# Leads per batch: another order for the same instructions in a four-layer graph network

## The chip, the cores and the metric

The kernel runs on one core of a Trainium2 chip. The core has five engines that this document names by their short forms: PE (TensorE, matrix multiplications; PEld is its weight load), DVE (VectorE), ACT (ScalarE), POOL (GpSimd) and SP (SyncE, which here issues most DMAs). Each engine works through its own list of instructions in the order in which it was written, and waits on semaphores for the others. The metric is the device time of one execution in microseconds (us): the median of several runs. A difference of 0.2% (about 5 us) is about the smallest that a measurement of this kernel can tell from none.

## The reference

Sixteen graphs (batches) of 1024 nodes with 128 features pass through four layers. Each layer normalises its input, applies a ReLU, runs a graph operation on the dense 1024 x 1024 adjacency matrix `adj`, and adds the result to its input `x`. All is in float32.

```python
# layer 0, three times (i = 0, 1, 2):
h = h @ W + b;  nh = h / norm(h);  cos = nh @ nh.T
h = (edge_weight * cos) @ h;  h = relu(h)          # no relu after the last
# layer 1:
y = relu(((1 + eps) * x + adj.T @ x) @ W1 + b1) @ W2 + b2
# layer 2: attention from two scores per node
alpha = tanh(s1[:, None] + s2[None, :]);  h = softmax(where(adj > 0, alpha, -1e15)) @ h
# layer 3: attention from h A h' (made symmetric), softmax over rows, then three gates
e = (h @ A) @ h.T;  e = e + e.T;  att = softmax(where(adj > 0, e, 0), axis=1) * adj
hp = relu(att @ h);  out = o * tanh(sigmoid(i * hp + f * x))
```

The products `cos` and `e` are symmetric: the kernel computes their upper blocks and mirrors the rest.

## The kernel before, in words

**Tiling.** The 1024 nodes are 8 blocks of 128 partitions; a half (columns 0 to 511 or 512 to 1023) fills one PSUM bank of 512 float32. For every batch, `turn` loads the adjacency as eight tiles `adjT`: the DMA brings 32 x 32 squares to their mirrored places (L880), DVE transposes within the squares (L888), ACT sums the rows (L891). Layer 1 also loads the plain rows (`adjL`).

**A square product.** In layers 0 and 3, `Square.row(j, s)` makes row block j of the product for half s in a PSUM tile `sq`: matmuls for the upper blocks (L761), and PE transposes of kept blocks for the lower ones (L771). `Square.keep` puts the upper blocks into `above`: on ACT (a copy, L793), or, for batches 1 to 13, on DVE for rows 0 to 3 of the second half (L783). In the latter case `send` writes the blocks to HBM (`by_hbm`) and reads them back transposed as `got`, which replaces the PE transposes of rows 4 to 7 in the first half. DVE then multiplies each half by the adjacency (`ew` in layer 0, L960; `e` in layer 3, L1178), and PE accumulates over j (`acc`, L823, or L834 where the nodes are wanted on partitions). In layer 3, a row also needs its maximum (L1190), an exponential on ACT (L1194) and a second multiplication by the adjacency (L1203) first.

**Between products** there are short chains over several engines: a projection `psP` (PE), a bias or scaling (DVE), a transpose `ps_hTn` (PE) and its eviction (ACT, L623); and in front of each layer a normalisation: statistics (DVE, L671, L680), a reciprocal root (POOL, L563), scaling of half the blocks on DVE (L699) and half on ACT (L706), transposes `ps_hT` or `ps_hnT` (PE). The last part of layer 3, `finish`, is a chain of gates; its two tanh passes over z are L1275 and L1276.

**What sets the order.** The kernel first registers all operations of all batches with a planner, `Plan`, each with engine, planned duration, batch, and the tiles that it reads and writes. `link` adds dependencies (two engines that touch one PSUM bank count as dependent, reads included) and gives every operation a rank: the due time of its batch (60 us apart, the last one 52), less the longest planned path behind it (`tail`), less a **lead**. `order` then replays the program: it takes the engine that can start something first and, of what that engine could start within 0.05 us of that, the operation of lowest rank. A larger lead so moves an operation forward in its engine's list and a smaller one moves it back. At most two batches beyond the oldest one may be under way on the engines, and the numbers of tiles are limited (POOLS, KINDS). The instructions are written in the resulting order, engine by engine, and are fixed from then on: on the chip, an engine does not pass over one that waits. The planner's durations are its own and are used for the order alone.

Operations form groups by a key: stage, engine, and the first tile written, such as "3 ACT z" (layer 3, ACT, tile z) or "00 ACT above" (layer 0, first product). Before the change, LEADS holds one lead for a group, and may hold others for the first two batches ("<0", "<1") and the last two (">1", ">0"): 551 numbers. Batches 2 to 13 share the group's lead.

**The constants.** `prepare` loads the parameters of the later layers through ACT's DMA queue, in pieces between other ACT work, and computes a few matrices from them; the second and third products of layer 0, and layer 1, wait for it.

Of the kernel before, what the change touches and what calls it, by code (L numbers as in the profile page):

```python
# [53 lines left out]
class Plan:  # L54
# [53 lines left out]
    def link(self):  # L108
# [23 lines left out]
        for o in reversed(self.ops):  # L132
            o.tail = o.us + max((s.tail + o.lat for s in o.succs), default=0.0)
            lead = self.leads.get(o.key + o.edge, self.leads.get(o.key, 0.0))
            o.rank = (self.deadline(o.batch) - o.tail - lead, o.seq)
# [87 lines left out]
def tile_adj_preln(  # L223
# [30 lines left out]
    B = x.shape[0]  # L254
# [71 lines left out]
    for load_it in first:  # L326
# [19 lines left out]

    LEADS = {
        "0 ACT hT": -1, "0 DVE hn": -8, "0 DVE mv": 42.5, "0 DVE nb": -20, "0 DVE st": -77.5, "0 PE ps": -72.5,
        "0 POOL rstd": -1, "00 ACT above": -10.5, "00 ACT hT": 95, "00 ACT hTn": -20.5, "00 ACT sq": -31,
        "00 DMA by": -13.5, "00 DMA got": 15.5, "00 DVE above": -135, "00 DVE ew": 79.5, "00 DVE h": -95.5,  # L350
        "00 DVE ss": -131.5, "00 PE acc0": -252.5, "00 PE ps": -142, "00 PE psP": -0.5, "00 PE sq": -18.5,
        "00 POOL rn": -129.5, "01 ACT above": 56, "01 ACT hT": 11.5, "01 ACT hTn": 15, "01 ACT sq": 15.5,
        "01 DMA by": 4.5, "01 DMA got": 18.5, "01 DVE above": 4.5, "01 DVE ew": 51.5, "01 DVE h": -2.5,
        "01 DVE ss": 16, "01 PE acc0": -164.5, "01 PE ps": 42, "01 PE psP": -5.5, "01 PE sq": -11,
        "02 ACT above": -2, "02 ACT hTn": -615, "02 ACT sq": -25.5, "02 DMA by": 63.5, "02 DMA got": 0.5,
        "02 DVE above": 43.5, "02 DVE ew": -232.5, "02 DVE ss": 79.5, "02 DVE x": -55.5, "02 PE acc0": -28.5,
        "02 PE ps": 12.5, "02 PE sq": 222, "02 POOL rn": -103, "1 ACT g": -33, "1 ACT hn": 66, "1 ACT y1": -7.5,
        "1 DMA adjL": -113, "1 DVE adjL": -21, "1 DVE hn": 1.5, "1 DVE mv": 237.5, "1 DVE nb": 46,
        "1 DVE st": -625.5, "1 DVE x": -0.5, "1 PE acc1": 4, "1 PE py": -167.5, "1 PE py2": 67,
        "1 POOL rstd": -43, "2 ACT e2": -24, "2 ACT h": 287.5, "2 ACT hfl": 53, "2 ACT hn": -13.5,  # L360
        "2 ACT hnT": 18, "2 ACT s1": -14, "2 DVE alone": -51.5, "2 DVE e2": 48.5, "2 DVE h": 20,
        "2 DVE hn": 48.5, "2 DVE hrow": -43.5, "2 DVE mv": -2.5, "2 DVE nb": 78, "2 DVE rden": 9.5,
        "2 DVE x": 10, "2 PE acc2": 108.5, "2 PE p1": -90, "2 PE pf": -26.5, "2 PE ps": 117.5, "2 PE psP": -315,
        "2 POOL rstd": 4.5, "3 ACT above": -19.5, "3 ACT e3": 96.5, "3 ACT gate": -185.5, "3 ACT h3T": 19.5,
        "3 ACT hn": -84.5, "3 ACT hnT": -9.5, "3 ACT hp": -5, "3 ACT hpT": 41, "3 ACT hs": 46.5, "3 ACT z": 25,
        "3 DMA by": -13.5, "3 DMA got": 0.5, "3 DMA z": -130.5, "3 DVE e3": -363.5, "3 DVE gate": 83,
        "3 DVE h": -111.5, "3 DVE hn": 69, "3 DVE mv": -2, "3 DVE nb": 147, "3 DVE st": -192, "3 DVE sum": 53.5,
        "3 DVE top": -84, "3 DVE z": -925, "3 PE acc3": -130.5, "3 PE pg": -18.5, "3 PE ps": 19,
        "3 PE psN": 114, "3 PE psP": 95, "3 PE sq": -0.5, "3 POOL rstd": -59, "3 POOL z": 0.5,
        "T ACT adjT": 1.5, "T DMA adjT": -140.5, "T DVE adjT": -391, "x DMA x": 54.5, "0 ACT hT <0": -2,  # L370
        "0 ACT hT >1": -4.5, "0 ACT hn <1": -4.5, "0 DVE hn <0": 8.5, "0 DVE hn <1": 8.5, "0 DVE hn >0": 15.5,
        "0 DVE hn >1": 1, "0 DVE mv <0": -4.5, "0 DVE mv <1": 113, "0 DVE mv >0": 47.5, "0 DVE mv >1": -25.5,
        "0 DVE nb <0": 101.5, "0 DVE nb <1": -62.5, "0 DVE nb >0": -49, "0 DVE nb >1": -18.5,
        "0 DVE st <0": -85, "0 DVE st <1": -73.5, "0 DVE st >0": -122.5, "0 DVE st >1": -32, "0 PE ps <0": 85.5,
        "0 PE ps <1": 36, "0 PE ps >0": -31, "0 PE ps >1": 40, "0 POOL rstd <0": -6.5, "0 POOL rstd <1": -26,
        "0 POOL rstd >0": -7, "0 POOL rstd >1": 15.5, "00 ACT above <0": -32, "00 ACT above <1": -88,
        "00 ACT above >0": -294, "00 ACT above >1": -3, "00 ACT hT <0": 147.5, "00 ACT hT <1": -7,
        "00 ACT hT >0": 21, "00 ACT hT >1": 161.5, "00 ACT hTn <0": -70.5, "00 ACT hTn <1": 119.5,
        "00 ACT hTn >0": -22, "00 ACT hTn >1": -11, "00 ACT params <0": -26, "00 ACT sq <0": -34,
        "00 ACT sq <1": 134.5, "00 ACT sq >0": -119, "00 ACT sq >1": -25.5, "00 DMA by <1": 0,  # L380
        "00 DMA got <1": 1, "00 DVE above <1": -197, "00 DVE ew <0": 180, "00 DVE ew <1": 13,
        "00 DVE ew >0": -125, "00 DVE ew >1": -147.5, "00 DVE h <0": -25.5, "00 DVE h <1": -4.5,
        "00 DVE h >0": 12, "00 DVE h >1": -50.5, "00 DVE params <0": 171, "00 DVE ss <0": 0,
        "00 DVE ss <1": -73.5, "00 DVE ss >0": -46.5, "00 DVE ss >1": -4, "00 PE acc0 <0": -39.5,
        "00 PE acc0 <1": -212, "00 PE acc0 >0": -327.5, "00 PE acc0 >1": -253.5, "00 PE params <0": 56.5,
        "00 PE ps <0": -18.5, "00 PE ps <1": -16, "00 PE ps >0": -32, "00 PE ps >1": -130.5,
        "00 PE psP <0": -2.5, "00 PE psP <1": 32, "00 PE psP >0": -22.5, "00 PE psP >1": -43,
        "00 PE sq <0": 28.5, "00 PE sq <1": 10, "00 PE sq >0": 3.5, "00 PE sq >1": 10, "00 POOL rn <0": -11,
        "00 POOL rn <1": -164.5, "00 POOL rn >0": -96.5, "00 POOL rn >1": -144, "01 ACT above <0": 113,
        "01 ACT above <1": -11, "01 ACT above >0": 65.5, "01 ACT above >1": 24, "01 ACT hT <0": -15,  # L390
        "01 ACT hT <1": -17.5, "01 ACT hT >0": 3.5, "01 ACT hT >1": -39, "01 ACT hTn <0": 16.5,
        "01 ACT hTn <1": -22, "01 ACT hTn >0": 68, "01 ACT hTn >1": 8, "01 ACT sq <0": 174,
        "01 ACT sq <1": -3.5, "01 ACT sq >0": -69, "01 ACT sq >1": 107, "01 DMA by <1": -9, "01 DMA got <1": 25,
        "01 DVE above <1": -5, "01 DVE ew <0": 140, "01 DVE ew <1": -13.5, "01 DVE ew >0": -9.5,
        "01 DVE ew >1": -34, "01 DVE h <0": -6, "01 DVE h <1": -6, "01 DVE h >0": -4.5, "01 DVE h >1": 43.5,
        "01 DVE ss <0": -13.5, "01 DVE ss <1": 1, "01 DVE ss >0": 17.5, "01 DVE ss >1": 106,
        "01 PE acc0 <0": -17, "01 PE acc0 <1": -31, "01 PE acc0 >0": 10.5, "01 PE acc0 >1": 25.5,
        "01 PE ps <0": 46, "01 PE ps <1": 51, "01 PE ps >0": -56, "01 PE ps >1": 82, "01 PE psP >1": 6,
        "01 PE sq <0": 0, "01 PE sq <1": -6, "01 PE sq >0": 23.5, "01 PE sq >1": -25, "02 ACT above >0": -3.5,
        "02 ACT hTn <0": -145.5, "02 ACT hTn <1": -452.5, "02 ACT hTn >0": -65.5, "02 ACT hTn >1": -373.5,  # L400
        "02 ACT sq <0": -8.5, "02 ACT sq <1": -43, "02 ACT sq >0": -58, "02 ACT sq >1": -22.5,
        "02 DMA by <1": 47.5, "02 DMA got <1": 4, "02 DVE above <1": 36.5, "02 DVE ew <0": -5,
        "02 DVE ew <1": -72, "02 DVE ew >0": -202.5, "02 DVE ew >1": -44, "02 DVE ss <0": 70,
        "02 DVE ss <1": 60.5, "02 DVE ss >0": 39, "02 DVE ss >1": 58, "02 DVE x <0": -115,
        "02 DVE x <1": -125.5, "02 DVE x >0": 0, "02 DVE x >1": -173.5, "02 PE acc0 <0": -46.5,
        "02 PE acc0 <1": -209, "02 PE acc0 >0": 0, "02 PE acc0 >1": -96.5, "02 PE ps <0": -241.5,
        "02 PE ps <1": -295.5, "02 PE ps >0": -48, "02 PE ps >1": -28, "02 PE sq <0": -33.5,
        "02 PE sq <1": -145, "02 PE sq >0": 89, "02 PE sq >1": 0.5, "02 POOL rn <0": 47.5, "02 POOL rn <1": -39,
        "02 POOL rn >0": -118.5, "02 POOL rn >1": -53, "1 ACT g <0": 23, "1 ACT g <1": 48, "1 ACT g >0": 25.5,
        "1 ACT g >1": -35, "1 ACT hn <0": 57.5, "1 ACT hn <1": 189, "1 ACT hn >0": -5.5, "1 ACT hn >1": -4.5,  # L410
        "1 ACT y1 <0": 10.5, "1 ACT y1 <1": 13.5, "1 ACT y1 >0": -26.5, "1 ACT y1 >1": 10.5,
# [58 lines left out]
    now = [0, ""]  # L470

    def op(engine, us, reads, writes, fn, port=False, lat=None):
        o = plan.op(engine, us, reads, writes, fn, now[0], port, lat)
# [904 lines left out]
    params = Buf(None, [], "params")  # L1378
# [57 lines left out]
```

## Time and profile before

| what | value |
|---|---|
| time, median of 3 runs | 2437.61 us (2435.33 to 2437.78) |
| span of the profiled execution | 2440.0 us |
| PE busy | 2389.2 us |
| DVE busy | 2106.2 us |
| ACT busy | 1288.3 us |
| POOL busy | 230.9 us |
| first matmul starts | 12.9 us |
| last matmul ends by the trace | 2429.4 us |

The page of the profile cuts the span into 40 slices of 61 us and gives each engine's busy share in tenths. The groups name a line and an engine, how many instructions it has, and what ended the idle time before them. The time-ordered view gives start, duration, engine and line of each instruction, the tile written and the tiles read, and in brackets the idle time of the engine before it with the instruction that ended the wait. Buffer numbers are left out of names. In the view of waits a row reads: engine, tile and line that waited, whom it waited for; microseconds in all, number of times, longest. A float32 matmul of the program appears as two records on PE.

### The profile page before, as it was taken

To read this page: it belongs to the slowest core of one execution; us is meant where nothing else is said; L and a number is where in the kernel's file an instruction comes from. 1 tells how busy PE (TensorE), PEld (TensorE's weight loads), DVE (VectorE), ACT (ScalarE), POOL (GpSimd) and SP (SyncE) were. 2 spreads that over 40 slices of the span, in tenths; PEclk is the share of its full clock that TensorE was granted. 3 is DMA by queue.
4 is the path that set the end of the run, shared out by engine and by line. 5 is a ranking of instruction groups with operands and counts; after the bars stand their busy time and mean duration, and the time that the engine had idled before them with its cause. 6 is when DMAs were issued, how large, how long until landed. Compare 5 with 4: busy or idle time off the path is not lost. (4 is left out here: it accounts for less than half of the span.)

```text
span 2440.0 us, 34840 instructions
## 1 busy us (share of the span) xinstructions
PE 2389.2 (98%) x11946; PEld 1588.9 (65%) x11946; DVE 2106.2 (86%) x5264; ACT 1288.3 (53%) x2404; POOL 230.9 (9%) x141
## 2 busy tenths in 40 slices
PE   6999999999999999999999999999999999999996
PEld 3568576675766757576575766757676575765763
DVE  5767989888998988999889998999989888897677
ACT  4425564644646455454644646455454655656275
POOL 1100010100101001011010100101011010101021
PEclk9999999999999999999999999999999999999999
DMA  8632837559296583946739296493946738054000
GB/s 127 131 96 43 147 78 139 126 93 178 54 160 132 85 158 78 159 109 114 160 75 182 58 153 134 87 162 68 162 116 105 164 78 156 18 87 95 25 2 18
DMA packets 1129473, 263.35 MB, mean 108 GB/s; under 512 B 971856, under 2 KB 1112912, under 8 KB 1129296
## 3 DMA queue, kind: packets, MB, share of 16 engines
q1 hardware_dynamic: 1108368, 251.73, 54.9%
q10 hardware_dynamic: 20928, 9.40, 1.4%
q8 instruction: 94, 1.54, 0.3%
q14 instruction: 83, 0.68, 0.1%
HBM read 198.14 MB, written 62.91 MB: 107 GB/s over the span
## 5 line engine op out<-in xcount | busy, mean ns | idle before, releaser
L960 DVE SCALAR_TENSOR_TENSOR ew<-sq,rn,adjT 128x512 f32<-128x512 f32 x612 | 432.0, 738 | 72.1 <-ACT above L793 37.4
L823 PE MATMUL acc<-ew,h 128*128 128x512 f32 x1024 | 481.5, 597 | 3.6 <-DVE ew L960 3.6
L761 PE MATMUL sq<-hTn 128*128 128x512 f32 (+3 forms) x1152 | 431.4, 487 | 0.3 <-ACT hTn L623 0.3
L793 ACT COPY above<-sq 128x256 f32<-128x256 f32 (+3 forms) x432 | 167.8, 393 | 439.0 <-PE sq L761 239.7
L761 PEld LDWEIGHTS sq<-hTn 128*128 128x128 f32 x1152 | 200.9, 191 | 153.2 <-issue 103.5
L823 PEld LDWEIGHTS acc<-ew,h 128*128 128x128 f32 x1024 | 179.8, 192 | 164.1 <-issue 124.1
L834 PEld LDWEIGHTS acc<-h,ew 128*128 128x128 f32 x2048 | 240.7, 192 | 23.0 <-issue 17.3
L834 PE MATMUL acc<-h,ew 128*128 128x128 f32 x2048 | 250.3, 276 | 0.0
L823 PE MATMUL acc<-e,hs 128*128 128x512 f32 x512 | 242.5, 598 | 5.6 <-DVE e L1203 4.4
L834 PEld LDWEIGHTS acc<-h,e 128*128 128x128 f32 x2048 | 232.9, 192 | 11.9 <-issue 6.5
L834 PE MATMUL acc<-h,e 128*128 128x129 f32 x2048 | 233.8, 275 | 1.2 <-DVE e L1110 1.2
L823 PE MATMUL acc<-adjL,hn 128*128 128x512 f32 x512 | 233.4, 593 | 0.3 <-ACT hn L727 0.3
L563 POOL TENSOR_TENSOR rstd<-ve,mhalf 128x8 f32<-128x8 f32 x64 | 105.1, 1642 | 1249.7 <-DVE ve L682 1197.6
L1194 ACT ACTIVATE e<-e,top 128x1024 f32<-128x1024 f32 x128 | 147.0, 1149 | 135.8 <-DVE top L1190 134.4
L771 PEld LDWEIGHTS sq<-ident,above 128*128 128x128 f32 x960 | 125.8, 141 | 135.4 <-issue 89.9
L891 ACT ACTIVATE adjT<-adjT 128x1024 f32<-128x1024 f32 x128 | 135.1, 1056 | 146.0 <-DVE adjT L888 109.4
L771 PE MATMUL sq<-ident,above 128*128 128x128 f32 x960 | 175.7, 274 | 9.7 <-ACT above L793 9.7
L888 DVE STREAM_TRANSPOSE adjT<-adjT 128x1024 f32<-128x1024 f32 x128 | 155.0, 1224 | 28.2 <-DMA adjT<-in_adj_dram 21.6
L706 ACT ACTIVATE hn<-x,nb,rstd 128x128 f32<-128x128 f32 x256 | 105.3, 483 | 123.6 <-DVE nb L690 117.8
L1110 DVE SCALAR_TENSOR_TENSOR e<-adjT,e 128x512 f32<-128x512 f32 x256 | 158.7, 679 | 9.3 <-ACT e L1106 8.8
L783 DVE STREAM_TRANSPOSE above<-sq 128x512 f32<-128x512 f32 x208 | 146.5, 706 | 17.2 <-PE sq L761 17.2
L1203 DVE TENSOR_TENSOR e<-e,adjT 128x512 f32<-128x512 f32 x248 | 161.0, 680 | 0.0
(130 smaller groups left out, 3493.8 us busy)
## 6 DMA issues: line engine op xcount, KB each, us to landing
adjT<-in_adj_dram SPq DMA_DIRECT2D x512, 128.0 KB, 4.0
adjL<-in_adj_dram SPq DMA_DIRECT2D x128, 512.0 KB, 5.2
by_hbm<-above SPq DMA_DIRECT2D x104, 512.0 KB, 4.0
got<-by_hbm SPq DMA_DIRECT2D x416, 128.0 KB, 3.8
x<-in_x_dram SPq DMA_DIRECT2D x15, 512.0 KB, 4.6
out_dram<-z ACTq DMA_DIRECT2D x15, 512.0 KB, 5.6
x<-in_x_dram SPq DMA_DIRECT2D x2, 256.0 KB, 5.1
out_dram<-z ACTq DMA_DIRECT2D x2, 256.0 KB, 2.3
```

The lines of the kernel that those rows point to most:

```text
L761: lambda: nc.tensor.matmul(dst.t[:, (first - lo) * P :], cols(leftT.t, j), span(rightT.t, first, hi), start=True, stop=True),
L771: nc.tensor.transpose(cols(dst.t, r), cols(above.t, p), ident)
L783: lambda: nc.vector.transpose(span(above.t, p, p + 4), read.t),
L793: lambda: nc.scalar.copy(span(above.t, p, p + hi - first), read.t[:, (first - lo) * P :]),
L823: lambda s=s, lo=lo, hi=hi: nc.tensor.matmul(acc[s].t, cols(h.t, at, w), span(ew.t, lo, hi), start=(j == 0), stop=(j == NB - 1)),
L834: nc.tensor.matmul(a.t[:, (c - lo) * n : (c - lo + 1) * n], cols(ew.t, c), h.t[:, at * w : at * w + n], start=(j == 0 and c == lo), stop=( ...
L888: dve(V(N), [t], [t], lambda t=t: nc.vector.transpose(t.t, t.t), True)
L891: lambda t=t, c=c: nc.scalar.activation(t.t, t.t, AF.Copy, accum_out=su.t[:, c : c + 1]),
L960: lambda view=view, ew=ew, rn=rn, j=j, lo=lo, hi=hi: nc.vector.scalar_tensor_tensor(by_block(span(ew.t, lo, hi), D, 4), view(), rn.t[:, j ...
L1110: lambda e=e, j=j, lo=lo, hi=hi: nc.vector.scalar_tensor_tensor(span(e.t, lo, hi), span(aT[j].t, lo, hi), 0.0, span(e.t, lo, hi), op0=ALU. ...
L1194: lambda e=e, top=top, tot=tot: nc.scalar.activation(e.t[:, 0:N], e.t[:, 0:N], AF.Exp, bias=top.t, accum_out=tot.t),
L1203: lambda e=e, j=j, lo=lo, hi=hi: nc.vector.tensor_mul(span(e.t, lo, hi), span(e.t, lo, hi), span(aT[j].t, lo, hi)),
```

## The change

The leads are now given for each batch by itself: a group's entry is a tuple of 16 numbers, 130 groups and so 2080 numbers. The edge suffixes go, as does the field that carried them. The values were found by simulated annealing on the planner's own replays with disturbed durations: an order is sought that stays good when operations take somewhat more or less time than planned. No operation, tile, pool or planned duration changes; only the ranks do, and with them the order of each engine's list. The DMA and constant loads are ranked by the same rule.

The diff, cut to its core (the list of leads is long; two groups of it are shown, the first of them for batches 14 and 15 in the edge entries before):

```diff
-            lead = self.leads.get(o.key + o.edge, self.leads.get(o.key, 0.0))
+            lead = self.leads[o.key][o.batch] if o.key in self.leads else 0.0
             o.rank = (self.deadline(o.batch) - o.tail - lead, o.seq)
...
     LEADS = {
-        "3 ACT z": 25, ... "3 ACT z >0": -17.5, "3 ACT z >1": -24,
-        "3 ACT above": -19.5, ... "3 ACT above >0": -12, "3 ACT above >1": -124.5,
...
+        "3 ACT above": (-52.5, -66, -4.5, -49, 47, 7, -1, 36.5, 0.5, -50, 42, -6, -64.5, -64, -105.5, -0.5),
+        "3 ACT z": (-65, 31, -54.5, -78, -69, -147.5, 23, -11.5, -36.5, -108, -18, -41.5, -81.5, -46, -141.5, -27.5),
...
-        o.edge = f" <{now[0]}" if now[0] < 2 else f" >{B - 1 - now[0]}" if now[0] > B - 3 else ""
```

Two places of the resulting orders are named in what follows (line numbers of the kernel before; in the kernel after, lines below the list stand nine lower). At the head, ACT's list before is L891 of tile 6, then the copy L793 of row 5; after, the copy comes first. At the tail, ACT's list before is the two z operations of batch 14 (L1275, L1276), then the copies (L793) of batch 15's layer-3 rows 0 and 1; after, the four copies come first. Before the last layer norm, DVE's list has two L1203 halves of batch 14 between the layer-2 result and the statistics; after, they stand ahead. There PE has six accumulations of batch 14 left to do before, and eight after.

## The prediction

> **What bounds the kernel now.** First the page's top rows: which engine is full, and when.
>
> ```profile
> span 2440.0 us, 34840 instructions
> ...
> PE 2389.2 (98%) x11946; PEld 1588.9 (65%) x11946; DVE 2106.2 (86%) x5264; ACT 1288.3 (53%) x2404; POOL 230.9 (9%) x141
> ...
> PE   6999999999999999999999999999999999999996
> ```
>
> TensorE (PE) is called busy 98% of the span, and only the first and last of the 40 slices (61 us each) show it idle. The ends of matmuls are modelled, so I measure work by pitch instead: the time from one start to the next when nothing waits. The time-ordered view gives it: the twelve 128x512 records below last 5.32 us, and less the 0.16 us by which the last one runs on, 5.16/12 = 0.43 us each.
>
> ```profile
> 2376.95 5.32 PE L823 MATMUL acc<-e,hs 128*128 128x512 f32 x12
> ```
>
> In the same way 128-wide matmuls come every 0.112 us, transposes every 0.109, 256-wide every 0.216, 384-wide every 0.323. Counts from the groups: 3008 records of 512 columns x 0.429 = 1290; 256 x 0.323 + 256 x 0.216 + 256 x 0.112 = 167; 6175 others of 128 to 131 columns x 0.112 = 692; 1984 transposes x 0.109 = 216. All together PE needs 2366 us. The span is 2440. So 74 us are not matmul work: 12.9 before the first matmul, 10.6 after the last, and 50.7 of lost pitch between. Cut by slices, the 50.7 are 20.6 in the first two slices, 17.9 in the last two (4.2 and 13.8), and 12.2 in the 2196 us between. An order can win only from these.
>
> Next the head, in order of time, engine by engine.
>
> ```profile
> 45.54 1.25 DVE L888 STREAM_TRANSPOSE adjT<-adjT 128x1024 f32<-128x1024 f32 x1 [4.21 <-DMA adjT<-in_adj_dram]
> ...
> 46.82 1.06 ACT L891 ACTIVATE adjT<-adjT 128x1024 f32<-128x1024 f32 x1 [5.53 <-DVE ss L947]
> ...
> 47.88 0.35 ACT L793 COPY above<-sq 128x256 f32<-128x256 f32 x1
> ...
> 48.28 0.47 PE L771 MATMUL sq<-ident,above 128*128 128x128 f32 x1 [6.45 <-ACT above L793]
> ...
> 59.16 1.25 DVE L888 STREAM_TRANSPOSE adjT<-adjT 128x1024 f32<-128x1024 f32 x1 [3.90 <-DMA adjT<-in_adj_dram]
> ...
> 63.71 1.01 PE L570 MATMUL ps_hT<-ident,hn 128*128 128x128 f32 x4 [1.38 <-DVE hn L699]
> ```
>
> The largest stall of the whole trace, 6.45 us, is a PE transpose waiting for an ACT copy (above, L793) that is ready to run but stands behind ACT's L891, which waits for an adjacency tile that DVE can transpose only when it has landed (45.5). The next tiles land at 59.2 and 62.1. Then the tail:
>
> ```profile
> 2386.07 1.66 PE L570 MATMUL ps_hnT<-ident,hn 128*128 128x128 f32 x8 [1.95 <-DVE hn L699]
> ...
> 2393.23 1.06 ACT L1275 ACTIVATE z<-z 128x1024 f32<-128x1024 f32 x1
> ...
> 2394.33 1.15 ACT L1276 ACTIVATE z<-z,half 128x1024 f32<-128x1024 f32 x1
> ...
> 2395.98 1.88 DVE L1178 SCALAR_TENSOR_TENSOR e<-adjT,sq 128x512 f32<-128x512 f32 x3 [4.69 <-ACT above L793]
> ```
>
> PE has run out of batch 14's work and waits 1.95 us for the last layer norm. Then DVE, which sets the last 40 us, sits idle 4.69 us for the ACT copy, and ACT spends the last 2.1 of these on batch 14's two z operations. Last, the waits:
>
> ```profile
> DVE ew L960 <- DMA got<-by_hbm: 13.9, 13, 3.1
> ```
>
> In the middle, DVE waits 13 times for blocks that return from HBM. The longest, 3.1 us at 751 us, is the one that PE feels most (1.8 us idle behind it).
>
> **What the Trainium skill says.** (1) "Perfetto Trace Analysis", Identifying the Most-Contended Engine: matmul busy time is a poor measure of headroom because matmuls are pipelined. Agreed: 98% is shown, while 2366/2440 = 97% is work and 23.4 of the 50.7 us lost do not show as idle. (2) "PSUM — Partial Sum Buffer", Engine vs sequencer instructions: the queues of ScalarE, VectorE and GpSimd are strict FIFO. Agreed: the copy at 47.88 ran only after 46.82. (3) Same page, PSUM bank collisions raise a hardware error: a dependency is needed even between ACT and DVE reads of one bank. Agreed: DVE's 4.69 us end with ACT's read of the same tile. (4) "DMA: Bandwidth & Descriptors", Specifications: under 512 B a transfer is below line rate. The page here counts 971856 of 1129473 packets under that size, and in the head tiles arrive 3 to 10 us apart.
>
> **The change part by part.** It removes and adds no instruction: both built orders hold the same matmuls, and my pitch sum is 2366 us for either. Only ranks move. 551 leads (one per group, others for the two first and two last batches) become 2080, one per group and batch. So I compare orders in three places.
>
> *Head.* Before, ACT has adjT tile 6 (L891) ahead of the copy of row 5; after, it has the copy first, so the 6.45 us wait at that transpose goes. What replaces it: PE's next tile-6 matmul needs tile 6 transposed (46.7) and multiplied (0.67), so it starts near 47.4. By pitch PE then finishes product 0 of batch 0, with one waiting group of transposes pulled in, near 53 instead of 57.3. But now the transposes of batch 2's input (ps_hT) come next, and their DVE input stands behind the tile that lands at 59.16: it is ready at 59.16 + 1.16 + 0.07 + 1.0 = 61.5. All that PE has queued waits behind it, 8 us. From there, adding up in the new order: ps_hT 0.44 and two squares 0.86 each to 63.8; second ps_hT, two more squares and a transpose to 65.8; batch 1's first accumulation to 66.7; two projections to 68.5; then no wait over 0.5 us until the constants are ready and batch 0's second product begins, near 77.3, with 46.7 us of matmul work done: 30.6 us lost. Before, the same point came at 80.99 with 47.6 done: 33.4 lost. Gain 2.8 us. Bounds: 0 if tiles land later (no order can hurry them, and the queue's order is the same), 5 if PE's waits after 61.5 vanish.
>
> *Tail, layer norm.* From batch 15's last layer-2 accumulation (2376.95) to its first normalised transpose before: 2386.07 - 2376.95 = 9.1 us, two L1203 halves of 0.60 in it. After, these stand ahead of the chain, so it is 7.9. PE covers it with 8 accumulations (6.88) and the psN projections (1.8) = 8.7 instead of 6 and 1.8. The 1.95 goes; DVE is up to 0.5 late at the tile before. Gain 1.7 (1.0 to 2.0).
>
> *Tail, z.* The two z operations move behind the first four copies. The first copy can start as soon as its square is done, about 1.5 to 2.3 us before 2395.4; the squares start 0.8 earlier too, since pg's second half moves behind the h3T transposes. The moved 2.1 us is hidden: DVE has four e halves (2.4) and two maxima (2.26) = 4.7 us of work, ACT four copies (2.0) + 2.1 + 0.55 = 4.65. I take 1.8 (0 to 2.5). The 27 us of DVE work that follow, then the end, are unchanged. Tail together 3.5.
>
> *Middle.* Round trips: DVE work between the last block sent and the first read back, in product 0, grows from 7.5 us to 8.0-9.3 in nine of the inner batches, more than the about 1 us that most of the 13 waits are. Against it, PE work covering the trip in product 2 shrinks from 15.5 to 12.8-13.7 us in batches 6, 9 and 13, and in product 1 from 23.4 to 13.5 in batch 3. New tight places on PE: an accumulation 0.1 us behind its square in batch 13 (its DVE step is 0.67 plus hand-overs), transposes right behind the copied square in batch 14, layer-3 squares right behind h3T in batches 2 and 4 (copy 0.6). Each costs 0.5 to 1.3, together about 4. Before has its own: 6.1 us of its 12.2 stand at eleven stalls. I take a gain of 1.5, bounds +6 and -6.
>
> Sum: 2.8 + 3.5 + 1.5 = 7.8; 2437.6 - 7.8 = 2430.
>
> **Rivals.** *Middle gives it back* (20%): the ends gain 4 to 6, the irregular middle loses as much, 2433 to 2441; taken as 2437. For it: the middle before repeats one pattern and loses only 12 us over 2196. Against: wider cover in nine batches. *Slower* (12%): a round trip that is late in a thinner batch blocks DVE, hence PE; six batches at 1.5 to 3.1 us (the 751 us case) minus the ends' gain gives 2443 to 2450. For it: DVE is 86% busy and in order. Against: 12.8 us of cover is near the 12 to 13 us after which most waits of before ended. *Larger gain* (18%): head 5, tail 4.5, middle 6: 2437.6 - 15.5 = 2422.
>
> **How the numbers follow.** The forecast, 2426 to 2432.7, has 50%. Faster by over 0.2% (below 2432.7) is this and the larger gain: 68%. Same is 20%, slower 12%. The range leaves out half of the larger gain's lower side and most of the slower case: 2421 to 2441.
>
> **What would show it.** Right: no PE wait of over 2 us at the above transposes near 48; a wait of about 8 ending near 61.5 at ps_hT; no wait at the last ps_hnT; DVE's idle before the first e of batch 15 near 3 instead of 4.69; pitch lost in the middle near 11. Wrong: tiles of batch 1 landing at other times, new DVE waits on got of over 3 us, or accumulations waiting for ew in batches 3, 6, 9 or 13.

## The result, and the profile after

| | median, us | against the kernel before on the same chip |
|---|---|---|
| before | 2437.49 (2435.33 to 2437.78, 4 runs) | |
| after | 2448.28 (2447.99 to 2449.15, 4 runs) | ratio 1.0047 [1.0029, 1.0064] |

The change made the kernel 10.8 us slower. The forecast was 2430, the range ended at 2441. All line numbers of the changed kernel in the parts concerned are 9 higher than before (L960 is L969, L823 is L832).

The page of the changed kernel, first rows:

```profile
span 2446.2 us, 34793 instructions
...
PE 2390.9 (98%) x11946; PEld 1587.6 (65%) x11946; DVE 2115.9 (86%) x5264; ACT 1283.2 (52%) x2404; POOL 232.0 (9%) x141
```

The instruction counts of the engines are those of before. DVE is busy 9.7 us longer (2106.2 before) with the same 5264 instructions. Since no instruction was added, some must have become longer; the middle below shows which. Before that, the accounts by pitch, worked out as in the prediction (start-to-start times less the undisturbed pitch, cut by slices of 61 us):

| lost pitch, us | head (slices 1, 2) | middle | last two slices | after the last matmul |
|---|---|---|---|---|
| before | 12.9 + 7.7 | 12.2 | 4.2 + 13.8 | 10.6 |
| after | 16.3 + 0.5 | 23.0 | 6.1 + 11.3 | 10.6 |

The head gained 3.8, the tail 0.6, and the middle lost 10.8. That is 6.4 us of loss in all, not 10.8: the profiled execution of the kernel before took 2441.8 us, 4.3 more than its median, that of the kernel after 2448.0, so sizes read from these two traces alone can be off by some 4 us. Nearly all of the middle's loss, 11.6 us, lies after 1281 us (2.1 before, 13.7 after).

Head, PE in order of time:

```profile
47.99 2.08 PE L832 MATMUL acc<-ew,h 128*128 128x512 f32 x2 [4.51 <-DVE ew L969]
...
60.23 1.01 PE L579 MATMUL ps_hT<-ident,hn 128*128 128x128 f32 x4 [1.89 <-DVE hn L708]
```

The 6.45 us wait at the transpose of above is gone. What took its place is spread: 4.51 us at an accumulation and only 1.89 us at ps_hT, which got its input at 60.2 and not at 61.5.

Tail, PE and DVE in order of time:

```profile
2374.72 9.68 PE L843 MATMUL acc<-h,e 128*128 128x129 f32 x80 [1.80 <-DVE e L1119]
...
2392.98 1.50 PE L579 MATMUL ps_hnT<-ident,hn 128*128 128x128 f32 x8
```

```profile
2401.06 0.69 DVE L1187 SCALAR_TENSOR_TENSOR e<-adjT,sq 128x512 f32<-128x512 f32 x1 [3.42 <-ACT above L802]
```

The last ps_hnT no longer waits, and DVE's idle time before the first e of batch 15 is 3.42 instead of 4.69. But 20 us earlier PE waits 1.80 us for a layer-2 e.

The waits of the whole span and then the groups, for the middle:

```profile
DVE ew L969 <- DMA got<-by_hbm: 15.8, 14, 2.3
...
PE acc L832 <- DVE ew L969: 13.2, 10, 4.5
...
PE pf L1074 <- DVE hrow L1067: 2.5, 2, 1.7
```

```profile
L969 DVE SCALAR_TENSOR_TENSOR ew<-got,rn,adjT 128x512 f32<-128x512 f32 x156 | 119.5, 797 | 21.8 <-DMA got<-by_hbm 15.8 <-issue 2.8 <-PE acc L843 1.7
```

DVE waits for blocks hardly longer than before (15.8 for 13.9). PE's waits for ew grew from 3.6 to 13.2 us, but half of that is the head, with the 4.51 us shown above; between 122 and 2318 us they grew from 2.6 to 6.6, and PE's wait of 2.5 us at the layer-2 product pf is new. And the 156 ew<-got take 797 ns each, where the same group before took 745: 8.8 us of DVE's 9.7. One such place, all engines in order of time:

```profile
1335.30 1.41 DVE L969 SCALAR_TENSOR_TENSOR ew<-got,rn,adjT 128x512 f32<-128x512 f32 x2 [2.26 <-DMA got<-by_hbm]
...
1336.63 0.17 DVE L1305 TENSOR_SCALAR gate<-gate 128x24 f32<-128x24 f32 x1
1336.71 3.06 DVE L969 SCALAR_TENSOR_TENSOR ew<-got,rn,adjT 128x512 f32<-128x512 f32 x2
1336.94 2.27 POOL L1316 TENSOR_TENSOR z<-hn,gate 128x1024 f32<-128x1024 f32 x1 [5.23 <-DVE gate L1305]
...
1340.48 1.12 PE L832 MATMUL acc<-ew,h 128*128 128x512 f32 x2 [2.50 <-DVE ew L969]
```

Two ew<-got in front of the gate operation take 1.41 us together, two behind it 3.06. The gate operation (batch 7) starts POOL's z multiply (z<-hn,gate, a step of `finish`), and the second of the two runs (2.39 us alone) until the multiply is over. The multiply too is longer, 2.27 instead of 1.91 us: it began inside the first one. PE then waits 2.50 us. The same place in the kernel before:

```profile
1333.63 0.18 DVE L1296 TENSOR_SCALAR gate<-gate 128x24 f32<-128x24 f32 x1 [2.02 <-ACT gate L1295]
...
1333.94 1.91 POOL L1307 TENSOR_TENSOR z<-hn,gate 128x1024 f32<-128x1024 f32 x1 [35.03 <-PE py L1022]
...
1338.34 2.74 DVE L960 SCALAR_TENSOR_TENSOR ew<-got,rn,adjT 128x512 f32<-128x512 f32 x4 [0.65 <-DMA got<-by_hbm]
```

There the multiply is over at 1335.85, before the four ew<-got start. Between the two, DVE has x<-py and st operations, and they keep their usual times.

The Trainium skill, "SBUF — State Buffer", section "SBUF: two separate sides", names this: DVE and GpSimd share a pair of SBUF ports under an exclusive lock, which counts for a DVE operation with two SBUF inputs (ew<-got reads got and adjT) against a GpSimd operation that reads SBUF, and the loser blocks fully. This trace agrees: 2.39 us for 0.74. Adding up every DVE instruction that overlaps one on POOL, less the median of its kind, gives 0.8 us before and 11.4 after; 8.2 of them are ew<-got beside the z multiply.

### The profile page after: what moved, and what is told of

Read it like the earlier page. It is cut to its first block, busy times and chain, and to the rows that moved or that the text cites. A ratio compares the mean times of both kernels' runs of the same rounds, so it can differ in the third digit from the quotient of the medians.

```text
span 2446.2 us, 34793 instructions
## 1 busy us (share of the span) xinstructions
PE 2390.9 (98%) x11946; PEld 1587.6 (65%) x11946; DVE 2115.9 (86%) x5264; ACT 1283.2 (52%) x2404; POOL 232.0 (9%) x141
## 4 chain that ended last, share of the span: by engine, by line
PE 79%; DVE 10%; DMA 5%; SPq 3%; ACT 2%; issue 1%; ACTq 0%; POOL 0%; DVEq 0%; POOLq 0%
PE acc L832 29%; PE acc L843 16%; PE sq L770 16%; PE psP L610 5%; PE sq L780 3%; DVE ew L969 3%; DMA by_hbm<-above 2%; DMA got<-by_hbm 2%; SPq L889 2%; PE py L620 2%; PE py L1031 2%; PE ps_hTn L579 1%; SPq L823 1%; DVE e L1187 1%; PE pg L620 1%; DVE top L1199 1%
## 5 line engine op out<-in xcount | busy, mean ns | idle before, releaser
L832 PE MATMUL acc<-ew,h 128*128 128x512 f32 x1024 | 482.7, 596 | 13.4 <-DVE ew L969 13.2
L969 DVE SCALAR_TENSOR_TENSOR ew<-sq,rn,adjT 128x512 f32<-128x512 f32 x612 | 432.6, 738 | 60.2 <-ACT above L802 28.2
L832 PEld LDWEIGHTS acc<-ew,h 128*128 128x128 f32 x1024 | 178.2, 191 | 174.3 <-issue 121.3
L832 PE MATMUL acc<-e,hs 128*128 128x512 f32 x512 | 243.6, 598 | 5.6 <-DVE e L1212 3.9
L832 PE MATMUL acc<-adjL,hn 128*128 128x512 f32 x512 | 232.8, 593 | 0.4 <-ACT hn L736 0.4
L1203 ACT ACTIVATE e<-e,top 128x1024 f32<-128x1024 f32 x128 | 146.9, 1148 | 133.3 <-DVE top L1199 132.5
```

What stands on the lines that cost most here:

```text
L832: lambda s=s, lo=lo, hi=hi: nc.tensor.matmul(acc[s].t, cols(h.t, at, w), span(ew.t, lo, hi), start=(j == 0), stop=(j == NB - 1)),
L969: lambda view=view, ew=ew, rn=rn, j=j, lo=lo, hi=hi: nc.vector.scalar_tensor_tensor(by_block(span(ew.t, lo, hi), D, 4), view(), rn.t[:, j ...
L1203: lambda e=e, top=top, tot=tot: nc.scalar.activation(e.t[:, 0:N], e.t[:, 0:N], AF.Exp, bias=top.t, accum_out=tot.t),
```

## The experiments

Two theories stood at first. **Lock:** the new order puts the gate operation of six inner batches directly ahead of or between the ew<-got of the batch after the next, and the blocked DVE work stalls PE. **Tightness:** the order is more irregular everywhere, DVE comes late with or without POOL. Later a third question came up, the blocks from HBM. Numbers after a dash are the median's difference from the kernel before on the same chip.

**Take the meeting away, and make it where it was not.** One instruction, and the multiply that it releases, moved in the finished order:

```diff
     ordered = plan.order()
+    def move(b, spot, behind):            # gate: second operation, then POOL's multiply
+        pair = [of(b, "3 DVE gate")[1], of(b, "3 POOL z")[0]]
...
+    for b in (4, 6, 8, 9, 11):            # e1, on the order after
+        move(b, of(b + 1, "2 DVE x")[0], 1)
+    for b in (7, 10):
+        move(b, read_back(b + 2)[0], 0)
...
+    for b in range(2, 12):                # e2, on the order before
+        move(b, read_back(b + 2)[1], 1)
```

> The changed kernel, with one DVE instruction moved in seven batches (and the POOL multiply it releases): the last gate operation, which lets POOL's z<-hn,gate start, no longer stands directly ahead of or between the four ew<-got operations, but ahead of the idle time before them (batches 7 and 10) or behind the x<-hn operations that follow them (4, 6, 8, 9, 11). Theory (POOL's multiply and DVE's operation with two SBUF inputs lock each other out): the ten long ew<-got and two long alone<-su shrink to 0.67 to 0.74 us each, DVE busy falls from 2116 to about 2107, most of the 8.3 us of PE stalls at those places go, and the time falls from 2448.3 to 2440 to 2442. Rival (the order is tighter everywhere and DVE comes late for other reasons, such as blocks back from HBM): the same places stall with another releaser, 2446 to 2449.

2441.24 — +3.5, ratio 1.0013 [1.0006, 1.0020]: 7 of the 10.8 us are back. One meeting stayed (batch 10, where the moved gate came no earlier), and the moved multiply now blocked other DVE operations instead, hrow and adjL of 128x128 (0.99 to 1.05 us for 0.27), so this is a lower bound for the lock.

> The kernel before, with the same instruction moved the other way in ten inner batches (2 to 11): the last gate operation and POOL's multiply stand between the second and the third ew<-got instead of some 5 us ahead of them. Nothing else is touched. Theory (lock): in each of the ten batches the third or fourth ew<-got takes about 2.4 instead of 0.74 us, POOL's multiply 2.27 instead of 1.91, DVE busy rises by 16 us, PE stalls 1 to 2.7 us in each, and the time rises by 10 to 25 us to 2448 to 2462. Rival (the order's tightness, not this meeting): one small operation moved by 5 us costs nothing, within 2 us of 2437.5.

2444.70 — +6.9, ratio 1.0026 [1.0015, 1.0038]. The same place of the old order, with the gate between the ew<-got:

```profile
1340.76 1.42 DVE L960 SCALAR_TENSOR_TENSOR ew<-got,rn,adjT 128x512 f32<-128x512 f32 x2 [0.18 <-DMA got<-by_hbm]
1342.09 0.17 DVE L1296 TENSOR_SCALAR gate<-gate 128x24 f32<-128x24 f32 x1
1342.17 3.06 DVE L960 SCALAR_TENSOR_TENSOR ew<-got,rn,adjT 128x512 f32<-128x512 f32 x2
1342.40 2.29 POOL L1307 TENSOR_TENSOR z<-hn,gate 128x1024 f32<-128x1024 f32 x1 [40.58 <-PE acc L823]
```

All ten ew<-got take 2.39 to 2.40 us, as expected, and DVE is busy 2120.0 us. The time rose by 7 and not by 10 to 25: PE's lost pitch grows from 50.7 to 57.6 us, 0.7 a meeting and never more than 1.2, where the four full meetings of the kernel after stand at stalls of 1.1 to 2.7. The mechanism is shown in both directions. Its size is not fixed: behind the same 1.65 us on DVE, PE loses from next to nothing to 1.2 us in this order.

**New ranks for some batches only.**

```diff
     def takes_after(key, b):
+        return b < 2                  # e3
+        return b < 2 or b > 13        # e4
```

> New leads for batches 0 and 1 alone; the old ones for all others, so that from batch 3 on the middle and the tail stand as before. Theory (head gains, middle loses, independently): the head's 4 us are gained, the middle loses nothing, 2433 to 2434. Rival (the earlier head only shifts batches against the DMA stream, and the middle pays for it): 2437 to 2442.

> New leads for batches 0, 1, 14 and 15; the old ones for 2 to 13. Theory: the head's 4 us and what the tail is worth by itself, 0.5 to 2.5 us: 2431 to 2433. Rival (the tail's loss of 1.9 us in the last slice but one comes with the new tail leads, not from the middle): 2433 to 2434, as with the head alone, and that slice loses about 6 us of pitch again. Second rival (the middle's loss comes from the ends): 2440 or more.

2484.46 — +46.7, and 2488.00 — +50.2: both theories missed. The loss is not in the head, which lost 16.9 us of pitch as in the kernel after, but between 305 and 671 us; that ranks made for another neighbour meet there is the likely reason, not a tested one. The second rival of e4, 2440 or more because the ends cost the middle, has the number, but e8 below has the same ends without such a loss. The e3 kernel, PE there, and the granted clock of a stretch of 10 us (the column PEclk is the last but two):

```profile
622.69 13.63 PE L968 MATMUL acc<-adjL,hn 128*128 128x512 f32 x24 [4.83 <-ACT hn L872]
```

```profile
622.00:632.00 10.00, 9.31 (x15) 4.00 (x16) 6.40 (x26) 0.64 (x2) 0.00 (x0) 0.66 1.06 237
```

The wait costs twice: 4.83 us, and after it matmuls that start every 0.85 us instead of 0.43. The Trainium skill, "TensorE: Matmul & The Clock Gate", Part 1, says that TensorE falls to half its clock when it has been idle for a window of some 3.4 us; this stretch agrees, 0.66 on average. So mixed leads tell nothing of the parts, and the parts had to be cut out of the finished orders instead.

**Cut and join.** The two orders issue the same set of operations at many places, and can be joined there without changing either part:

```diff
+    new, old = planned(LEADS), planned(OLD)
...
+    i, k = cut(125), cut(2331)
+    ordered = joined((new, 0, i), (old, i, len(old)))                     # e5
+    ordered = joined((old, 0, k), (new, k, len(old)))                     # e6
+    ordered = joined((old, 0, i), (new, i, k), (old, k, len(old)))        # e7
+    ordered = joined((new, 0, i), (old, i, k), (new, k, len(old)))        # e8; e15 with cut(1290) for cut(125)
```

> Both orders are worked out and joined at a place where they have issued the same operations: the new order up to about 130 us, the old one from there. Theory (the three stretches are independent): the head's gain of 4 us alone, 2433 to 2434. Rival (the head's gain is given back by what follows it, whatever the order there): 2436 to 2438.

> The old order up to about 2330 us, the new one from there to the end. By the prediction the tail is worth 3.5 us: 2434. By the trace of the changed kernel it is worth 0.6, since the last slice but one loses 1.9 us more: 2437, with a wait of about 1.8 us for a DVE e operation near 2370, which POOL's multiply of e lengthens. If the 1.9 us were a late effect of the middle, not of the tail's own order: 2434 to 2435.

> The old order up to about 130 us and from about 2330 us on, the new one between. Theory: all of the loss is here, 10.9 us of pitch: 2447 to 2450, with the same ten long ew<-got. Rival (the loss needs the earlier head, which shifts the middle against the blocks from HBM): 2440 to 2444.

> The new order up to about 130 us and from about 2330 us on, the old one between. Theory: head 4.1 and tail 0.6 to 2.5 gained, nothing lost: 2431 to 2433, below both kernels, and no ew<-got over 0.8 us. Rival (a join costs what the ends gain): 2436 to 2440.

| part that is new | median, us | difference | ratio [95%] |
|---|---|---|---|
| e5 head | 2432.62 | −6.4 | 0.9970 [0.9959, 0.9982] |
| e6 tail | 2436.79 | −2.3 | 0.9992 [0.9985, 0.9998] |
| e7 middle | 2452.79 | +13.7 | 1.0054 [1.0041, 1.0067] |
| e8 head and tail | 2430.36 | −8.7 | 0.9961 [0.9948, 0.9973] |

The middle is the culprit, and it doesn't need the new head for that. Head and tail add up in e8, which beats both kernels. e7 has its nine long DVE operations where the kernel after has them (six ew<-got, and not the ten that the expectations count, two alone<-su and one hrow). Head, tail and middle sum to +5 while the change as a whole measured +10.8; the 10.8 alone has an interval of 7.1 to 15.6, so the gap may be no more than noise.

**Take POOL's multiply out.** Everything keeps its place, and the multiply is not issued; DVE's next operation adds x where it added the product:

```diff
-    lambda: nc.gpsimd.tensor_mul(part(z), part(hn), per_node(of(1), n)),
+    lambda: nc.gpsimd.tensor_mul(part(z), part(hn), per_node(of(1), n)) if late else None,
...
-    scaled(hp, D if by_nodes else E3, 0, z)
+    scaled(hp, D if by_nodes else E3, 0, z, z if late or final else xt)
```

> The changed kernel without POOL's z multiply in batches 0 to 13: the gated hn is left out of the output, and DVE adds x in its place; everything else stands in the same order. Theory (lock): the ten long ew<-got, two alone<-su and the hrow all return to their usual lengths, DVE busy falls by about 10 us, the loss between 1281 and 2318 us falls from 13.7 to 3 to 5, and the time falls from 2448.3 to 2437 to 2440. Rival (tightness): it falls by 1 us at most from where moving the gate left it, 2440 to 2442, and the loss of 7.7 us that stayed there stays.

> Control: the kernel before without the same multiply (the gated hn is left out of the output, DVE adds x). There POOL's multiply runs beside operations that it does not block, so by the theory nothing is gained: within 2 us of the kernel before. If POOL's time in the chain of z itself mattered, it would be faster by up to 13 x 0.2 us = 2.6 us or more.

2438.75 — +1.7, ratio 1.0007 [1.0001, 1.0014], and the control 2436.97 — −0.1, ratio 1.0001 [0.9993, 1.0009]. So the lock costs the new order 10.8 − 1.7 = 9.1 us, give or take some 4, and the old one nothing. But e9 stays 10 us above e8, which has the same ends: the lock is about half of the middle's loss. The group in e9 is back at its usual length, and DVE still waits for got:

```profile
L969 DVE SCALAR_TENSOR_TENSOR ew<-got,rn,adjT 128x512 f32<-128x512 f32 x156 | 111.4, 746 | 21.4 <-DMA got<-by_hbm 14.2 <-issue 5.0 <-PE acc L843 0.6
```

**The multiply on ACT.**

```diff
+    def of_x_on_act():
+        for k in range(lo, hi):
+            nc.scalar.activation(cols(z.t, k), cols(hn.t, k), AF.Copy, scale=gate.t[:, 3 * k + 1 : 3 * k + 2])
...
-    lambda: nc.gpsimd.tensor_mul(part(z), part(hn), per_node(of(1), n)),
+    of_x_on_act if b < 13 else lambda: nc.gpsimd.tensor_mul(part(z), part(hn), per_node(of(1), n)),
```

> The changed kernel with the z multiply of batches 0 to 12 done by ACT in eight 128x128 operations of about 0.40 us (3.2 us a batch) instead of by POOL in one; the result stays the same. Theory (lock): the DVE operations return to their usual lengths as when it is left out; ACT is 53% busy, but its copies stand in order behind the eight operations: 2439 to 2445. Rival (ACT's copies matter more than the lock): 2448 or more.

2449.77 — +12.7, ratio 1.0056 [1.0042, 1.0069]. The rival holds: DVE's lengths are back (2106.8 us busy), yet nothing is won, since PE now waits 0.7 to 2.3 us at transposes of above, whose ACT copies stand behind the eight operations. One of them, ACT and PE in order of time:

```profile
1932.93 2.45 ACT L1308 ACTIVATE z<-hn,gate 128x128 f32<-128x128 f32 x8 [0.89 <-DVE gate L1305]
...
1935.85 0.35 ACT L802 COPY above<-sq 128x256 f32<-128x256 f32 x1
1936.26 0.33 PE L780 MATMUL sq<-ident,above 128*128 128x128 f32 x1 [2.13 <-ACT above L802]
```

ACT is 54% busy; being in order counts, not the share.

**What is the other half?** First PE's list: in batches 9 to 11 the second accumulation of tile 4 stands right behind what feeds it.

```diff
+    for b in (9, 10, 11):
+        behind(step(b, 4, 1), step(b, 5, 0))
+    for b in (12, 13):
+        behind(pf, step(b, 4, 1))
```

> As the kernel without POOL's z multiply (the gated hn left out of the output, x added in its place), and with one PE operation moved in five places: in batches 9 to 11 the second accumulation of tile 4, which needs the ew<-sq that DVE makes just behind the four ew<-got, stands behind the first accumulation of tile 5 (as in the old order); in batches 12 and 13 the pf product, which needs hrow, stands behind that accumulation. Second cause proposed: what is left of the middle's loss when the lock is gone is PE's list, which gives DVE too little time between a square and its accumulation; the waits of 1.0, 0.7, 0.9 and 0.9 us there go, and the time falls from 2438.8 to 2434.5 to 2436. Rival (DVE is late there because blocks come back late from HBM, whatever PE's order): the waits turn up at the next operation that needs DVE, 2438 to 2439.5.

2439.54 — +2.0, ratio 1.0008 [1.0001, 1.0014]. Nothing is won. In its trace PE's waits for ew between 1281 and 2318 us fall from 4.5 to 1.6 us of pitch, but the largest one there is now 1.18 us at a pf product. (The trace of e9 is of an execution of 2440.8 us, that of e12 of one of 2436.3; the medians decide.) The position of these five isn't the cause; DVE is late.

Then the blocks from HBM. e13 (without the multiply, new order) and e14 (new ends, old middle) read them from an input, so that no read waits for a store:

```diff
-    src = by_hbm.t.rearrange("(x j) (g i) -> g j x i", j=SQ, i=SQ)
+    src = x[0].rearrange("(x j) (g i) -> g j x i", j=SQ, i=SQ)
```

> As the new order without POOL's z multiply (the gated hn left out of the output, x added instead), and with the blocks that come back from HBM read from the input x instead of from where they were just stored: the same transfers in the same order, but none waits for a store. This leaves out which block is read back. If the rest of the middle's loss is the round trip (new order sends later or reads earlier), DVE's waits for got vanish and the time falls from 2438.8 by 6 to 9 us to 2430 to 2433, level with e14. If the rest is the order of PE and DVE among themselves, it falls by 0 to 3 us to 2436 to 2439.

> Control: new ends, old middle, with the blocks read back from the input x instead of from where they were stored (which block is read back is left out). The old middle waits little for them: 2427 to 2430, from 2430.4.

> The new order up to about 1290 us and from 2331 us on, the old one between. By the traces the first half of the new middle loses 8 us and the old one 7, and nearly all of the difference lies after 1281 us: 2430 to 2433. If the first half took part in the loss: 2435 or more.

2438.37 — −0.6, ratio 0.9998 [0.9990, 1.0006]; 2429.58 — −9.4, ratio 0.9961 [0.9949, 0.9974]; and for the place 2431.34 — −7.7, ratio 0.9969 [0.9958, 0.9980]: the loss is all after 1290 us. That e13 gained only some 2 us looked like the end of the blocks theory. The queue says otherwise. The last block of batch 10, product 0, in e9, then in e13:

```profile
1467.59 0.82 SPq L812 DMA_DIRECT2D by_hbm<-above  x1
...
1471.82 2.73 SPq L823 DMA_DIRECT2D got<-by_hbm  x4
...
1479.41 2.74 DVE L969 SCALAR_TENSOR_TENSOR ew<-got,rn,adjT 128x512 f32<-128x512 f32 x4 [1.19 <-DMA got<-by_hbm]
```

```profile
1466.15 0.84 SPq L812 DMA_DIRECT2D by_hbm<-above  x1
...
1468.03 5.80 SPq L823 DMA_DIRECT2D got<-in_x_dram  x4
...
1478.17 2.74 DVE L969 SCALAR_TENSOR_TENSOR ew<-got,rn,adjT 128x512 f32<-128x512 f32 x4 [0.79 <-DMA got<-in_x_dram]
```

Without the wait for the store the four reads start 1.9 instead of 4.2 us after the send, but their issue takes 5.80 instead of 2.73 us, and ends 7.7 us after the send, against 7.0. DVE still waits. The experiment had not taken away what it was meant to. So DVE was taken off the blocks altogether:

```diff
+    still = const.tile([P, HALF], F32, name="still")
...
-    return self.got, lambda: self.got.t.rearrange("p (r c d) -> p c r d", r=QUARTER, d=P)[:, q]
+    return self.got, lambda: still.rearrange("p (c d) -> p c d", d=P)
```

> The new order without POOL's z multiply (gated hn left out, x added instead), and with DVE's ew<-got and e<-got operations reading a constant tile of the same shape; the blocks are still sent and read back, but nothing waits for them (their values are left out of the output). If what remains of the middle's loss is waiting for blocks to land, the time falls from 2438.8 to 2430 to 2433. If it is the order of DVE's and PE's own work, 2436 to 2439.

> Control: new ends and old middle with the same constant tile in place of the blocks that come back (their values are left out): DVE waited 7 us for them in all, PE hardly: 2427 to 2430.

> As e16 (without POOL's z multiply, with a constant tile in place of the blocks that come back), with the five PE operations moved back as in e12. If PE's positions count once DVE is in time: 2 to 4 us below e16. If not: level with e16 within 1 us.

2432.40 — −5.1, ratio 0.9979 [0.9971, 0.9988]; control 2429.79 — −7.7, ratio 0.9967 [0.9955, 0.9980]; with PE's moves 2433.03 — −4.5, ratio 0.9982 [0.9974, 0.9990]. In the e16 trace the same DVE group waits for no transfer:

```profile
L971 DVE SCALAR_TENSOR_TENSOR ew<-still,rn,adjT 128x512 f32<-128x512 f32 x156 | 111.2, 745 | 1.2 <-PE acc L845 0.9
```

The new order gains 1.7 + 5.1 = 6.8 us from it and the old one nothing (e8 2430.36, e17 2429.79). The blocks were taken away only where the multiply was gone too, so the two shares hold in this order of removal. PE's five moves bring nothing here either.

## Why the prediction was wrong

The sum, from new ends with the old middle (e17) to the kernel after: 10.8 + 7.7 = 18.5 us. The lock is 9.1 of them, waiting for blocks 6.8, and 2.6 are left between e16 and e17. The terms come from different chips, each with an interval of some 2 to 5 us either way. For the 2.6 the traces have two places. One is in batch 13, where an accumulation stands right behind its square; in e9:

```profile
1883.72 1.98 PE L832 MATMUL acc<-ew,h 128*128 128x512 f32 x4 [0.80 <-DVE ew L969]
```

There and 3 us later PE loses 1.3 us of pitch, in every trace with the new order at this place (e16 too) and in none with the old one. The other is the head: e16 loses 2.2 us more than e17 in the first two slices, although PE, DVE and ACT have the same lists there, so this is not the order of the middle. No run tests either.

*Head* (forecast 2.8, bounds 0 to 5): right in direction, too small if anything. The trace of the kernel after shows 3.8, e5 measured 6.4 [4.4 to 10.0]. The place of the new wait was wrong: the 8 us at ps_hT became 4.51 us at an accumulation and 1.89 at ps_hT.

*Tail* (forecast 3.5): right in direction, too large. e6 measured 2.3 [0.5 to 3.7]. Both named waits went as described. The mis-sized term is "The 27 us of DVE work that follow, then the end, are unchanged": from the first e to the last accumulation 33.4 us before became 34.6, and the last slice but one lost 1.9 more, behind e operations of layer 2. In one of these, at 2373.18, two DVE operations take 2.08 instead of 1.28 us beside POOL's multiply of e.

*Middle*: this is the step that failed. "I take a gain of 1.5, bounds +6 and -6" was a loss of 13.7 by itself (e7). Two things were missed. First, the step weighed DVE's and PE's lists and never asked what runs on POOL at the same time: the new order has the gate operations of batches 4 and 6 to 10 in front of or between the ew<-got of the batch after the next. POOL, 9% busy, has no term in the sum. Its multiply cost 9.1 us. Second, "DVE work between the last block sent and the first read back ... grows from 7.5 us to 8.0-9.3 in nine of the inner batches" was taken as better cover. It was not enough: DVE is ready 10.6 us after the send in the example above (1479.41 − 1.19 − 1467.59), the block 11.8 after. The waits on got are hardly longer than in the old order; what changed is what PE has left when they come: between 122 and 2318 us of e6, which is the old order there, DVE waits 13.4 us for got and PE 0.9 for ew; in e9 it is 14.2 and 4.2. In e8, with the old middle, DVE can wait 1.85 us there and PE no more than 0.53:

```profile
1328.12 2.74 DVE L1105 SCALAR_TENSOR_TENSOR ew<-got,rn,adjT 128x512 f32<-128x512 f32 x4 [1.85 <-DMA got<-by_hbm]
1328.93 1.12 PE L968 MATMUL acc<-ew,h 128*128 128x512 f32 x2 [0.53 <-DVE ew L1105]
```

Of the tight places listed on PE ("about 4" us), the accumulation behind its square in batch 13 cost the 1.3 us above, the top of the 0.5 to 1.3 forecast for each; the five that e12 and e18 moved are others, and moving them proved worthless. And the 12.2 us that the middle loses before were those of one execution: in the traces of e5, e6, e8 and e10, with the old middle, it loses 7 to 10.

*Rivals*: the one named "Slower" had the time (2443 to 2450) and half of the cause, late blocks. It had them in products 1 and 2, where PE's cover shrank; the stalls came mostly in product 0, where DVE's cover had grown. The lock was in none of the four cases, so that the time fell into this rival's span is in part luck. The sign of error "accumulations waiting for ew in batches 3, 6, 9 or 13" came true in 9 (the 2.50 us above, the longest of the middle), 13 and, with 0.66 us of pitch, 6; 10 and 11, with the meeting too, were not named. Waits on got of over 3 us, another sign, did not come: the longest is 2.3.

Open: the 2.6 us, as far as the two places don't hold it; whether e5, e6 and e7 add up to the change; why reads without a wait for the store are issued so much more slowly.

## What to carry to other kernels

When an order changes, list for every GpSimd operation which VectorE operations it will run beside, before and after: an engine that is 9% busy set half of this loss. A wait moved on one engine is priced by what its consumer still has queued, not by its length: ten blockings of 1.65 us cost 6.9 us in one order (e2), and nine, most of them shorter, about as much or more in the other (9.1, e9). And two orders of one plan can be cut and joined where they have issued the same set, which sizes each stretch by itself, and here gave a kernel faster than both (2430.36); mixing their ranks does not.

## What the runs showed of the hardware

- Blocked beside the 128x1024 multiply on POOL: 128x512 ew<-got with two SBUF inputs (2.39 for 0.74 us), but also operations with one tensor input, hrow (0.99 for 0.27) and even a 128x8 TENSOR_SCALAR (alone<-su, 1.51 for 0.17); the page quoted above counts operations in a two-port mode in. Not blocked: ew<-sq, whose first input is in PSUM (0.74 to 0.75), and the st statistics.
- POOL's 128x8 rstd takes 1.64 us and blocks next to nothing: at 160.3 us of the kernel before, three ew<-got run beside it at 0.74 to 0.76 us each. The same page has the lock held for the whole instruction; here the length on POOL isn't what counts.
- Idle TensorE is paid for afterwards: 4.83 us of wait, then 0.85 us instead of 0.43 per matmul for some 6 us.
